# Forty residual additions of the second batch, moved from GpSimd instructions into accumulating transfers

## The chip, the cores and the metric

The kernel runs on one core of a Trainium2 chip. A core has five engines that run side by side, each with its own in-order queue of instructions: PE (TensorE, matrix products), DVE (VectorE), ACT (ScalarE), POOL (GpSimd) and SP (SyncE, which here only issues transfers). Sixteen DMA engines move data; any of the queues can issue to them, and PT<-Phl in the profile is a transfer that transposes on its way. The metric is device time in microseconds (us) for one execution, as the median of several runs.

## The reference, cut to what matters

The program is two layers over an input `x` of 2 batches x 1024 rows x 512 columns, in float32. In each layer an attention and a second branch both read a layer norm of `x`, and both results are added to `x`:

```
xn = layernorm(x)
x  = x + attn0(xn) + ffn0(xn)     # ffn0: four streams of 128 columns, mixed
xn = layernorm(x)
x  = x + attn1(xn) + ffn1(xn)     # attn1: 32 causal heads in 8 groups; ffn1: low-rank experts
```

The second branch of layer 0, `ffn0`, is what the change touches. Each row of 512 is seen as four streams of 128 columns. A small matrix `H_res` of 4x4 per row (made by 50 Sinkhorn steps) mixes the streams, and one branch result `y` of 128 columns is handed out to all four streams by weights `H_post`:

```
x_mixed[i]       = sum over j of H_res[i, j] * x_streams[j]
y_distributed[i] = y * H_post[i]
ffn0             = x_mixed + y_distributed
```

So for a block of 128 rows the residual gets one addition of 128x512 for `y_distributed`, and one addition of 128x512 for each of the four values of `j`.

## The kernel before

The rows are cut into 16 blocks of 128: `NT = 8` blocks for each of the two batches. The residual of block `t` of batch `b` stays on the chip for the whole program as `acc[b, t]`, 128 partitions x 512 float32. Products are done in float16 with a high and a low part, three passes for each (`mm3`, line 86).

The order of the whole program is: layer 0 of batch 0; layer 0's attention of batch 1; then layer 1, whose attention is one long loop (`layer1_attn`, line 807) over 16 groups (8 of batch 0, then 8 of batch 1) of 32 row steps each. Work that batch 1 still owes layer 0 is laid into the first groups of that loop with `put(h, s, f)` (line 1121), which gives a unit of work its row step. The program text sets the priorities; a list scheduler with a model of the time then writes the order of each engine's queue and places the semaphores and buffers. Two helpers correct it: `tc.issue_after` orders one engine's instructions, and `behind(i, j, True)` (line 195) makes instruction `i` wait for instruction `j` of another engine.

A row step (`row_step`, line 347) is the softmax of 128 rows: PE writes scores into PSUM (tile `s`), DVE subtracts a maximum (lines 292 and 296, tile `P`), ACT takes the exponential (line 300), DVE and ACT make the scale `r` (lines 324 and 325), ACT writes the high part (line 330, tile `Phl`) and DVE the low part (line 338, `Phl<-P,r,Phl`). The last DVE instruction of that kind is remembered in `last_low[0]`. POOL clears what is left of the tile (line 342), and SP issues the transposing transfer (line 343, `PT<-Phl`), which PE needs for the product with the values (line 373, tile `av`).

POOL does three other things in the loop. It issues the fetches of weights from HBM (`fetch`, line 715, into a tile tagged `f2k`); it splits them into high and low parts (`split_pool`, lines 97 to 99, `f2k` to `wq` or `wo`), each first instruction behind `last_low[0]`; and in the first part of the loop it does a Sinkhorn chain for batch 1 (lines 569 to 577, tile `sk`). Tiles tagged `f2k` share four buffers.

The additions of `ffn0` to the residual are done in two functions.

`branch0_add` (line 473) makes the 128x512 product of `y` and its four weights on POOL (line 477, into an `f2k` tile), and adds it to `acc[b, t]` on POOL (line 481). For batch 1 it is put at row steps 8, 10, ... 22 of the first group. The product, not the addition, is behind `last_low[0]` there.

`mix0_units` (line 624) does the mixing of one block: `load` fetches the input rows again into an `xr` tile and normalises them (on POOL at line 645 for batch 1), and four calls of `stream` follow, one for each `j`. With `pool` true (always for batch 1, four of the eight blocks of batch 0) ACT scales stream `j` four times into the four quarters of an `f2k` tile `m` (line 661), and POOL adds `m` to `acc[b, t]` (line 662). For batch 1 that addition too is behind `last_low[0]`. The units of batch 1 start at row steps 122 to 193 of the loop:

```
for t in range(NT):
    for k, f in enumerate(mix0_units(1, t, f0[1][5], True)):
        put(0, MX0 + MXN * (4 * t + max(k - 1, 0)) // 32, f)
```

What reads `acc[1, t]` next is the layer norm's statistics (`norm_stats`, line 217: DVE, line 219, `bnst<-acc`), once for each block, and later the normalised copy. In the same row steps the additions of layer 1's attention go to `acc[0, t]` (DVE, line 777), so they touch other blocks.

Of the kernel before, what the change touches and what calls it, by code (L numbers as in the profile page):

```python
# [12 lines left out]
ALU = mybir.AluOpType  # L13
# [41 lines left out]
def tile_model(ctx: ExitStack, tc: tile.TileContext, out: bass.AP, a: dict):  # L55
# [3 lines left out]
    V, A, G = nc.vector, nc.scalar, nc.gpsimd  # L59
# [7 lines left out]
    def T(tag, shape, dt=F32, bufs=None):  # L67
        count[0] += 1
        kw = {} if bufs is None else {"bufs": bufs}
        return sb.tile(shape, dt, tag=tag, name=f"{tag}_{count[0]}", **kw)  # L70
# [4 lines left out]
    def PP(shape=(P, 512)):  # L75
        count[0] += 1
        return ps.tile(list(shape), F32, tag="pp", name=f"pp_{count[0]}", bufs=BP)

    def bc(ap, axis, n):
        return ap.unsqueeze(axis).to_broadcast(  # L80
            [*ap.shape[:axis], n, *ap.shape[axis:]])
# [43 lines left out]
    acc = {}  # L125
# [60 lines left out]
    last_hi, last_lo, last_low = [None], [None], [None]  # L186

    def after(*insts):

        st = ExitStack()  # L190
        for i in insts:
            st.enter_context(tc.issue_after(i.ins))
        return st

    def behind(i, j, wait=False):

        kind = mybir.DependencyClass.Sync if wait else mybir.DependencyClass.NoSync
        tc.add_manual_dep(i.ins, j.ins.name, mybir.DependencyInfo(
            kind, mybir.DependencyReason.DATA), reason="behind")

    def rsqrt(y, ve, tag):

        t = T(tag, list(ve.shape), bufs=2)
        A.activation(t, ve, AF.Ln)
        A.activation(y, t, AF.Exp, scale=-0.5)
        V.tensor_tensor(t, y, y, ALU.mult)
        V.tensor_tensor(t, t, ve, ALU.mult)
        V.tensor_scalar(t, t, -0.5, 1.5, ALU.mult, ALU.add)
        V.tensor_tensor(y, y, t, ALU.mult)
# [51 lines left out]
    def srow():  # L261
        count[0] += 1
        return ps.tile([P, 512], F32, tag="s", name=f"s_{count[0]}", bufs=BS)
# [68 lines left out]
    def rows_lo(Pm, r, W, pool, hl, dst):  # L332
        whole, hi, los, pad = hl
        for a0, a1, lo in los:
            if pool:
                G.tensor_tensor(lo, Pm[:, a0:a1], hi[:, a0:a1], ALU.subtract)
            else:
                last_low[0] = V.scalar_tensor_tensor(lo, Pm[:, a0:a1], r[:, 1:2], hi[:, a0:a1],  # L338
                                                     ALU.mult, ALU.subtract)
        if pad is not None:  # L340

            behind(G.memset(pad, 0.0), last_low[0])  # L342
        nc.sync.dma_start_transpose(dst[:, :whole.shape[1] // P], whole)
# [129 lines left out]
    def branch0_add(b, t, y4, hh):  # L473

        y = y4
        y4 = T("f2k", [P, 4, P], bufs=FB)
        mul = G.tensor_tensor(y4, bc(y, 1, 4), bc(hh[:, t, 1, :], 2, P), ALU.mult)
        if b:
            behind(mul, last_low[0], True)
        af = acc[b, t]  # L480
        G.tensor_tensor(af, af, y4.rearrange("p i c -> p (i c)"), ALU.add)

    def attn0_rows(b, half, Q, K, between=lambda: None):
        PTs = []
# [139 lines left out]
    def mix0_units(b, t, rs, pool):  # L624


        got = {}

        def load():
            if b == 0 and t >= 4:  # L630
                if t % 2 == 0:
                    xr_more[t] = T("P", [P, 2, H], bufs=PB)
                xr = got["xr"] = xr_more[t & ~1][:, t % 2]
            else:
                xr = got["xr"] = T("xr", [P, H], bufs=XB)
            with after(t0):
                nc.sync.dma_start(xr, a["x"][(b * NT + t) * P:(b * NT + t + 1) * P, :])
            if b == 0:
                A.activation(xr, xr, AF.Identity, scale=rs[:, 2, t:t + 1], bias=rs[:, 1, t:t + 1])
                if not pool:  # L640
                    got["d"] = srow() if t < 4 else PP()
                    A.activation(got["d"], acc[b, t], AF.Copy)
                return
            with tc.issue_after(p0.ins):
                behind(G.tensor_scalar(xr, xr, rs[:, 2, t:t + 1], rs[:, 1, t:t + 1], ALU.mult, ALU.add),
                       last_low[0], True)

        def stream(j):
            if b == 0 and (not pool or j > 1):
                with after(*(last_rs[:1] if pool else last_rs[1:] if j else last_mix)):  # L650
                    stream_at(j)
            else:
                stream_at(j)

        def stream_at(j):
            xj = got["xr"][:, j * P:(j + 1) * P]
            by = [Hm[b][:, t, i, j:j + 1] for i in range(NC)]
            if pool:
                m = T("f2k", [P, H], bufs=FB)
                for i in range(NC):  # L660
                    A.activation(m[:, i * P:(i + 1) * P], xj, AF.Copy, scale=by[i])
                add = G.tensor_tensor(acc[b, t], acc[b, t], m, ALU.add)
                if b:
                    behind(add, last_low[0], True)
                return

            for i in range(NC):
                sl = slice(i * P, (i + 1) * P)
                dst = acc[b, t] if j == NC - 1 else got["d"]
                last_stt[0] = V.scalar_tensor_tensor(dst[:, sl], xj, by[i], got["d"][:, sl], ALU.mult, ALU.add)  # L670

        return [load] + [lambda j=j: stream(j) for j in range(NC)]
# [389 lines left out]
    for t in range(NT):  # L1062
        branch0_add(0, t, ys0[t], f0[0][4])
# [71 lines left out]
    for t in range(NT):  # L1135
        put(1, 2 * t, lambda t=t: branch0_add(1, t, y4s[t], f0[1][4]))
# [93 lines left out]
```

## Time and profile before

| what | us |
|---|---|
| median of 3 runs | 1851.93 (1847.24 to 1852.3) |
| the profiled execution's own time | 1847.82 |
| its span, first to last instruction | 1846.1 |
| PE busy | 1708.1 (93%) |
| DVE busy | 1473.8 (80%) |
| ACT busy | 1189.0 (64%) |
| POOL busy | 871.5 (47%) |

The batch 1 additions lie in two stretches. Those of line 481 start between 284.7 and 324.8 us, those of line 662 between 618.7 and 837.4 us. In the profile a line of a group reads: line, engine, operation, output tile <- input tiles, shapes, count | busy us, mean ns of one | idle time of the engine before them and what ended it. A line of the waits reads: who waited, at which line <- for whom: us in total, times, longest. A line of the stretches has the length of the stretch, then busy us and count for each engine, then TensorE's granted clock, the share of time that the DMA engines were busy, and GB/s. In the timeline a line has the start, the duration and the instruction. A DMA line ends with the us from issue to landing.

### The profile page before, as it was taken

Reading aid. Unit: us, or ns where it says so; the run is one execution under the profiler, and the core shown is the slowest. Engines: PE = TensorE matmul, PEld = TensorE weight load, DVE = VectorE, ACT = ScalarE, POOL = GpSimd, SP = SyncE. Lnnn points to the kernel's source line nnn. Section 1 sums busy time; section 2 is a strip of 40 time slices with the busy share of each in tenths; the row PEclk is TensorE's granted clock in tenths of the full one; section 3 lists DMA queues with packets and bytes.
Section 4 is the critical chain, followed back from the end, with each engine's and each line's share of the span. In section 5 each row is a group of like instructions: output and inputs, shape, how many; then the busy total and the mean of one; then the engine's idle time right before and its main releaser. Section 6 shows DMA issues by size and latency. Waiting matters only on the chain. (4 is left out here: it accounts for less than half of the span.)

```text
span 1846.1 us, 35011 instructions
## 1 busy us (share of the span) xinstructions
PE 1708.1 (93%) x11394; PEld 1038.2 (56%) x11394; DVE 1473.8 (80%) x4170; ACT 1189.0 (64%) x2917; POOL 871.5 (47%) x1460
## 2 busy tenths in 40 slices
PE   4666399999999999999999999999999999999998
PEld 2434146566666655566555566665666665665565
DVE  7988868888888877887577798898787877778675
ACT  3848656767665767886366667657566767666564
POOL 5568628878766464647254233324142323235200
PEclk9888699999999999999999999999999999999999
DMA  7435225756565656456484656557565665666455
GB/s 212 84 54 130 61 64 113 162 109 142 112 145 102 147 116 143 100 133 147 82 166 99 131 110 141 111 128 162 142 141 125 142 123 129 130 143 126 103 118 118
DMA packets 685034, 228.15 MB, mean 124 GB/s; under 512 B 665633, under 2 KB 665761, under 8 KB 684850
## 3 DMA queue, kind: packets, MB, share of 16 engines
q1 hardware_dynamic: 669394, 178.65, 47.2%
q0 software_dynamic: 13152, 43.07, 8.3%
q10 hardware_dynamic: 2304, 4.20, 0.7%
q8 instruction: 89, 1.46, 0.3%
q14 instruction: 95, 0.78, 0.2%
HBM read 52.81 MB, written 4.19 MB: 31 GB/s over the span
## 5 line engine op out<-in xcount | busy, mean ns | idle before, releaser
L300 ACT ACTIVATE P<-P,nm 128x1024 f32<-128x1024 f32 (+31 forms) x528 | 391.4, 742 | 278.1 <-DVE nm L292 253.4
L338 DVE SCALAR_TENSOR_TENSOR Phl<-P,r,Phl 128x64 f16<-128x64 f32 (+16 forms) x627 | 462.9, 763 | 79.0 <-ACT Phl L330 73.3
L91 PE MATMUL s<-K,Q 128*128 128x512 f16 (+22 forms) x2400 | 440.5, 317 | 19.8 <-DVE nm L292 10.5
L373 PE MATMUL av<-PT,V 128*128 128x256 f16 x3456 | 422.6, 273 | 12.2 <-DMA PT<-Phl 6.8
L373 PEld LDWEIGHTS <-V 128*128 128x128 f16 x3456 | 336.8, 98 | 95.1 <-DMA PT<-Phl 9.7
L330 ACT ACTIVATE Phl<-P,r 128x1024 f16<-128x1024 f32 (+31 forms) x515 | 368.8, 731 | 17.1 <-DMA PT<-Phl 2.0
L91 PE MATMUL pp<-wo,ao 128*128 128x512 f16 x1536 | 370.2, 380 | 3.3 <-ACT ao L107 3.2
L91 PE MATMUL pp<-big,wq 128*128 128x512 f16 x1536 | 368.6, 380 | 0.0
L97 POOL TENSOR_SCALAR f2k<-f2k 128x512 f32<-128x512 f32 x164 | 110.5, 675 | 512.3 <-DVE Phl L338 461.4
L91 PEld LDWEIGHTS <-Q 128*128 128x128 f16 x2400 | 223.9, 98 | 177.3 <-issue 29.6
L91 PEld LDWEIGHTS <-wq 128*128 128x128 f16 x1536 | 149.1, 98 | 166.8 <-issue 2.7
L91 PEld LDWEIGHTS <-ao 128*128 128x128 f16 x1536 | 149.7, 98 | 158.4 <-ACT ao L107 5.0
L91 PEld LDWEIGHTS <-big 128*128 128x128 f16 x1824 | 120.9, 99 | 87.8 <-DMA big<-wo 40.6
L292 DVE CUSTOM_DVE_ANT_0 P<-s,mask,nm 128x272 f32<-128x272 f32 (+15 forms) x256 | 157.7, 617 | 11.1 <-PE s L91 3.1
L296 DVE TENSOR_SCALAR_CACHE_REDUCE P<-s 128x512 f32<-128x512 f32 (+15 forms) x272 | 152.3, 562 | 11.9 <-PE s L91 10.4
L324 DVE RECIPROCAL r<-r 128x1 f32<-128x1 f32 x528 | 79.3, 155 | 78.6 <-ACT P L300 75.4
L325 ACT ACTIVATE r<-r 128x1 f32<-128x1 f32 x528 | 94.9, 192 | 68.3 <-DVE r L324 67.6
L107 ACT ACTIVATE ao<-av 128x512 f16<-128x512 f32 x128 | 75.0, 586 | 83.9 <-PE av L373 80.6
L342 POOL MEMSET Phl<- 128x192 f16 (+1 forms) x320 | 55.7, 189 | 153.0 <-DMA PT<-Phl 86.8
L292 DVE CUSTOM_DVE_ANT_0 P<-s,mask 128x32 f32<-128x32 f32 (+15 forms) x256 | 105.1, 430 | 19.0 <-PE s L91 18.6
L91 PE MATMUL pp<-big,big 128*128 128x128 f16 (+2 forms) x816 | 103.9, 283 | 17.5 <-DVE sk L606 12.7
L777 DVE SCALAR_TENSOR_TENSOR acc<-pp,acc 128x512 f32<-128x512 f32 x128 | 87.1, 681 | 31.6 <-PE pp L91 31.1
(266 smaller groups left out, 2064.3 us busy)
## 6 DMA issues: line engine op xcount, KB each, us to landing
f2k<-in_Wq POOLq DMA_DIRECT2D x64, 256.0 KB, 3.1
f2k<-in_WoT POOLq DMA_DIRECT2D x64, 256.0 KB, 3.3
PT<-Phl SPq DMA_TRANSPOSE x528, 3.2
acc<-in_x SPq DMA_DIRECT2D x16, 256.0 KB, 5.3
f2k<-in_Wup POOLq DMA_DIRECT2D x16, 256.0 KB, 3.4
xr<-V SPq DMA_DIRECT2D x32, 128.0 KB, 2.3
out<-acc ACTq DMA_DIRECT2D x16, 256.0 KB, 2.7
xr<-in_x SPq DMA_DIRECT2D x12, 256.0 KB, 5.1
```

What stands on the lines that cost most here:

```text
L91: nc.tensor.matmul(dst, lhs(l), rhs(r), start=(i == 0 and j == 0), stop=(i == n - 1 and j == 2))
L97: first = G.tensor_scalar(stage, stage, scale, 1.0, ALU.mult, ALU.mult)
L107: A.activation(hl_hi, src, AF.Copy, scale=scale)
L292: last_row[0] = V.tensor_tensor_reduce(Pm[:, o:o + w], pt[:, :w], mask[:, 512 - w:], -scale, first, ALU.add, ALU.min, nm[:, k:k + 1])
L296: last_row[0] = V.tensor_scalar(Pm[:, o:o + w], pt[:, :w], -scale, first, ALU.mult, ALU.min, accum_out=nm[:, k:k + 1])
L300: A.activation(Pm[:, :W], Pm[:, :W], AF.Exp, bias=last, scale=-1.0, accum_out=r[:, 0:1])
L324: V.reciprocal(r[:, 1:2], r[:, 0:1])
L325: A.activation(r[:, 1:2], r[:, 1:2], AF.Copy, scale=PSCALE)
L330: A.activation(hl[1], Pm[:, :W], AF.Copy, scale=r[:, 1:2])
L338: last_low[0] = V.scalar_tensor_tensor(lo, Pm[:, a0:a1], r[:, 1:2], hi[:, a0:a1], ALU.mult, ALU.subtract)
L373: nc.tensor.matmul(p, v, pt, start=(k == 0), stop=(k == len(todo) - 1))
L777: V.scalar_tensor_tensor(acc[b, t], p, 1.0 / 256.0, acc[b, t], ALU.mult, ALU.add)
```

## The change

A helper `add_to(dst, src)` issues a transfer from POOL's queue that adds `src` to `dst` where `dst` lies (both are on the chip). For batch 1, the addition of line 481 and the four additions of line 662 become such transfers: 8 + 32 = 40 in all, each 128 partitions x 512 float32 (256 KB). The wait of line 662's addition for the last low part goes with it; the product of line 477 keeps its own. Batch 0's additions stay POOL instructions, and the additions of the attention outputs stay on DVE.

```diff
+    def add_to(dst, src):
+
+        return G.dma_start(dst, src, accum_op=ALU.add)
+
     def rsqrt(y, ve, tag):
...
         if b:
             behind(mul, last_low[0], True)
-        af = acc[b, t]
-        G.tensor_tensor(af, af, y4.rearrange("p i c -> p (i c)"), ALU.add)
+        y4 = y4.rearrange("p i c -> p (i c)")
+        if b:
+            add_to(acc[b, t], y4)
+        else:
+            G.tensor_tensor(acc[b, t], acc[b, t], y4, ALU.add)
...
                     A.activation(m[:, i * P:(i + 1) * P], xj, AF.Copy, scale=by[i])
-                add = G.tensor_tensor(acc[b, t], acc[b, t], m, ALU.add)
                 if b:
-                    behind(add, last_low[0], True)
+                    add_to(acc[b, t], m)
+                else:
+                    G.tensor_tensor(acc[b, t], acc[b, t], m, ALU.add)
                 return
```

## The prediction

> **What bounds the kernel now.** I read the busy times and slices of the page first, then its chain, then stretches of the span, then the groups, waits and timeline of the stretch that the change touches.
>
> ```profile
> PE 1708.1 (93%) x11394; PEld 1038.2 (56%) x11394; DVE 1473.8 (80%) x4170; ACT 1189.0 (64%) x2917; POOL 871.5 (47%) x1460
> ...
> PE   4666399999999999999999999999999999999998
> ...
> PE 29%; DVE 3%; issue 1%; DMA 1%; ACT 1%; DVEq 0%; ACTq 0%
> ```
>
> From about 250 us on PE is the bound. A saving elsewhere counts only as far as it closes PE's holes. POOL is nowhere in the chain.
>
> ```profile
> core 0: us, PE busy (x) PEld busy (x) DVE busy (x) ACT busy (x) POOL busy (x), PEclk, DMA share, GB/s
> 280.00:330.00 50.00, 49.17 (x334) 30.49 (x333) 42.42 (x106) 33.08 (x82) 47.19 (x73) 1.00 0.57 125
> 400.00:617.00 217.00, 215.36 (x1419) 133.08 (x1418) 178.48 (x509) 141.55 (x338) 146.91 (x329) 1.00 0.59 122
> 617.00:840.00 223.00, 213.52 (x1501) 132.93 (x1499) 177.35 (x460) 174.59 (x472) 124.02 (x179) 1.00 0.60 132
> ```
>
> The mixing of batch 1 is the third stretch. PE misses 223.00 - 213.52 = 9.5 us there, against 217.00 - 215.36 = 1.6 in the one before: 7.8 more. In the first stretch (the branch sums) it misses 0.8. So 9.5 + 0.8 = 10.3 us is the most that these stretches can give back.
>
> ```profile
> L662 POOL TENSOR_TENSOR acc<-acc,f2k 128x512 f32<-128x512 f32 x32 | 42.9, 1342 | 61.9 <-DVE Phl L338 55.9 <-DVE r L324 4.0 <-ACT f2k L661 2.0
> ```
>
> ```profile
> PE s L91 <- DVE nm L292: 3.7, 4, 1.4
> PE av L373 <- DVE ao L108: 3.3, 2, 2.0
> ```
>
> These are the group of the 32 additions and PE's two longest waits between 617 and 840 us. With 0.6 more for DVE (`Q`) and 1.8 for ACT, 7.6 of 9.4 us are DVE's. POOL stood idle 59.9 us ahead of the additions, for DVE. The next lines are DVE's low parts alone (line 338) in the two long stretches, and the timeline at 750 us.
>
> ```profile
> 400.00:617.00 217.00, 61.06 (x72) 1.00 0.59 122
> 617.00:840.00 223.00, 72.85 (x72) 1.00 0.60 132
> ```
>
> ```profile
> 750.89 3.10 DVE L338 SCALAR_TENSOR_TENSOR Phl<-P,r,Phl 128x192 f16<-128x192 f32 x1
> 751.17 1.26 POOL L662 TENSOR_TENSOR acc<-acc,f2k 128x512 f32<-128x512 f32 x1
> ...
> 754.46 0.44 DVE L338 SCALAR_TENSOR_TENSOR Phl<-P,r,Phl 128x224 f16<-128x224 f32 x1
> ```
>
> The same 72 instructions take 11.8 us longer beside the additions. One of 192 columns took 3.10 us beside an addition and other POOL work; one of 224 took 0.44 without. The last lines are about transfers: three kinds and the software queue, and what follows a block's last addition.
>
> ```profile
> f2k<-in_Wq POOLq DMA_DIRECT2D x64, 256.0 KB, 3.1
> ...
> acc<-in_x SPq DMA_DIRECT2D x16, 256.0 KB, 5.3
> xr<-V SPq DMA_DIRECT2D x32, 128.0 KB, 2.3
> ```
>
> ```profile
> q0 software_dynamic: 13152, 43.07, 8.3%
> ```
>
> ```profile
> 837.39 1.26 POOL L662 TENSOR_TENSOR acc<-acc,f2k 128x512 f32<-128x512 f32 x1
> 839.43 0.68 DVE L219 BATCH_NORM_STATS2 bnst<-acc 128x6 f32<-128x512 f32 x1
> ```
>
> **The change, part by part.** The sum is made against the profiled execution, 1847.8 us (span 1846.1 and 1.7 around it), 4.1 below the median of 1851.9. I add the same difference to the median.
>
> *POOL's own time.* 32 additions (42.9 us) and 8 (11.4 us between 280 and 330) go; 40 issues come, at 0.59 us (the weight fetches on the same queue): 23.6. POOL is 30.7 us freer, worth nothing by itself: between 617 and 840 it is idle for 99 us, and around 300, where it has 47.19 of 50, PE has 49.17 of 50 all the same. Should an accumulating issue cost more than a fetch, the same idle time covers it: three times 0.59 for 32 would be 38 us more.
>
> *DVE's relief.* The low parts should lose up to 11.8 us. What a microsecond of DVE is worth at the end: 11.8 more of it stand beside 7.8 more of PE's holes, 0.66. But ACT also has 33 us more work there (174.6 against 141.6; the 128 scalings of line 661 are 40.3 and stay), so I give DVE half, 0.33: -3.9. Around 300 I take half of 0.8: -0.4. Bounds: 0 and -10.3.
>
> *When a transfer lands.* The trace shows no accumulating transfer. From below: 2.3 us (half the bytes, on the chip). From above: 8.2, the slowest of the loads into `acc`. I take 4.2, by the nearest row: a fetch of the same bytes on the same queue lands after 3.1 to 3.4, and a second read adds 0.9 (the software queue's 8.3% of 1846 us, over about 164 transfers). An addition took 1.3.
>
> *The wait that comes.* The four additions of a block change the same tile, so each waits on POOL until the one before has landed, and DVE's statistics wait for the last (as the first layer's wait for the loads into `acc` today: 8.2 us, 8 times). Today the statistics start 0.04, 2.6, 0.5, 0.4, 3.3, 1.2, 0.04 and 0.8 us after the last addition of their block. Block 4: additions at 736.6, 746.4, 748.4 and 751.2, statistics at 755.7. With 4.2 for each, the third goes at 750.6, the fourth at 754.8 and lands at 759.0, so DVE stands for 3.2 us, and the softmax queued behind with it. Over the eight blocks that makes 21.2 us if the transfers start where the additions do and DVE's order stays. If they start when ACT has written `m` (3.3 to 15.4 us earlier for the last of a block, as the wait for the low part is gone), it is 3.5 us. I take the middle, 12.4, times 0.33: +4.1. Bounds: 0 (2.3 us to land, early start) and 102 x 0.66 = +67 (8.2 to land, late start). The compiled order may put the statistics later by itself; nothing in the trace shows how far.
>
> *What is queued behind on POOL.* The waits inside a chain block POOL for 17.5 us (late start) to 78 (early), within its 99 idle plus the 24 freed there (42.9 less 18.9). Behind it stand the clearing of `Phl` (55 in this stretch), weight splits and fetches. The clearing holds up SP's transposes, and they PE; PE waited 0 for a transpose there and PEld 0.4, so there is room: +1.0, between 0 and +10 (at 8.2 us a chain blocks 109, beyond the idle time).
>
> *Buffers.* `m` is held from ACT's last write to the end of the addition: 6.3 us of waiting on average plus 1.3. A transfer without that wait holds it for 4.2 plus its chain, much the same; ACT waited 0.9 us for it. 0, bounds -0.9 and +5 (one more wait of 1.3 for every fourth of 32, half of it reaching PE).
>
> *The DMA engines.* 32 transfers at 2 x 0.9 us of sixteen engines are 60 in 223 us: the share goes from 0.60 to at most 0.87, beside the transposes. In slices with a share of 0.7 PE is at 9 tenths as in the others. 0, up to +3 if a transpose gets a microsecond later and one in 24 counts.
>
> [...] In the trace the additions follow each other on one engine, with a single wait of 0.2 us between two; no row shows what an overlap would lose. [...]
>
> Sum: -3.9 - 0.4 + 4.1 + 1.0 = +0.8. On the profiled run 1848.6, on the median **1852.7**: no change. About 0.3% (5.6 us) is what a measurement of this kernel can tell from none.
>
> **The rivals.**
> *Relief in full.* DVE's 11.8 us count at 0.66 and the holes around 300 close (-8.6), and every transfer lands ahead of its statistics. For it: POOL's 59.9 us of waiting goes, and ready streams were held 6.3 us. Against: ACT's load stays. 1843.3.
> *DVE waits for the landing.* If a transfer takes 5.3 us, as a load into `acc` does, the late start gives 40.4 us of waiting: 13.3 at 0.33, less 4.3, plus 1.0: +10.0, 1861.9; at 0.66 1875. It decides from where the relief of 4.3 is eaten (13 us of waiting) and is over 0.3% from 27 us, which is a landing of about 4.5 at a late start. For it: seven of eight statistics start within 3 us of the addition's end. Against: the early start.
> *The compiled order moves.* Different modelled durations may shift any queue after 285 us. After 850 PE's holes are 17.0 us (996 less 979.0); half of that either way is 1843 to 1860. Nothing in the trace decides it.
>
> **How the numbers follow.** No change 0.38; relief 0.21; late landing 0.29; moved order 0.12 (0.04 faster, 0.02 same, 0.06 slower). Faster 0.25, same 0.40, slower 0.35. The forecast's own range is 1846.4 to 1857.5. The range reaches from the bound of the relief (1851.9 - 10.3, rounded: 1842) to late landings between the two prices (1870); about 0.05 below and 0.12 above are left out.
>
> **What would show it.** Right: line 338 near 61 us for its 72 instructions while the streams are added; POOL down by some 30 us; statistics waiting for a DMA on `acc`, some 10 us in all; landings near 4.2; PE still at 9 in every slice. Wrong: landings over 5, DVE waits above 27 us, ACT waiting for `f2k`, or PE's holes moved to another stretch.

## The result, and the profile after

The changed kernel takes **1892.76 us** (median of 4 runs, 1890.38 to 1893.15) against 1850.77 for the kernel before (4 runs, 1847.24 to 1852.3). The ratio is **1.0227, 95% interval 1.0209 to 1.0245**: 42 us slower, where no change was forecast, and above the range. The profiled execution took 1890.38 us, its span 1888.6.

Lines of the page of the changed kernel: engines, PE by fortieths of the span, the chain, the new transfers (KB each, us from issue to landing) and the software queue.

```profile
PE 1723.8 (91%) x11394; PEld 1043.3 (55%) x11394; DVE 1456.4 (77%) x4170; ACT 1189.5 (63%) x2917; POOL 844.5 (45%) x1460
...
PE   4766389999999889898999999999999999999998
...
q0 software_dynamic: 18912, 53.56, 12.1%
...
PE 27%; DVE 2%; issue 1%; ACT 1%; DVEq 0%; ACTq 0%
...
acc<-f2k POOLq DMA_DIRECT2D x40, 256.0 KB, 4.0
```

POOL and DVE have become freer by 27.0 and 17.4 us, and the kernel slower. PE's slices show where: the new 8s, but for one near 240 us, stand between 610 and 900 us. Two stretches of the changed kernel, the first of all engines, the second of DVE's low parts alone (line 342, which was 338):

```profile
core 0: us, PE busy (x) PEld busy (x) DVE busy (x) ACT busy (x) POOL busy (x), PEclk, DMA share, GB/s
621.00:882.00 261.00, 228.29 (x1502) 138.18 (x1501) 165.57 (x470) 174.56 (x471) 108.69 (x183) 0.94 0.74 147
```

```profile
621.00:882.00 261.00, 58.09 (x73) 0.94 0.74 147
```

The same matrix products that took 223 us (617 to 840) now take 261. PE's holes there are 261.00 - 228.29 = 32.7 us (9.5 before), and the products themselves take 228.3 us instead of 213.5, at a granted clock of 0.94 instead of 1.00. So of the 38 us some 23 are holes and 15 are a lower clock. The low parts did lose what they lost to the additions: 72.85 us for 72 became 58.09 for 73.

From here on "the stretch" is one fixed piece of work in every kernel: the 1499 matrix products from the end of PE's 3323rd to the end of its 4822nd, worked out from the traces. It is 223.1 us before and 261.0 after. By the spans of the two profiled executions (42.5 us apart), 3.6 us more are lost ahead of it and 1.0 behind it. The 3.6 are there before the first moved addition: at PE's 1001st product (264.5 us before) the changed kernel is 5.8 us late.

The longest waits of the changed kernel between 617 and 875 us (who, at which line, for whom: us in all, times, longest):

```profile
PE s L91 <- DVE nm L296: 9.2, 5, 3.1
PE s L91 <- DVE Q L108: 4.0, 1, 4.0
...
DVE bnst L223 <- DMA acc<-f2k: 32.3, 8, 7.1
...
ACT P L304 <- DVE nm L296: 36.0, 12, 9.2
ACT f2k L668 <- DMA acc<-f2k: 18.9, 8, 5.8
...
POOL acc L203 <- DMA acc<-f2k: 29.6, 7, 5.8
```

Three engines now wait for a landing: DVE with all eight statistics, POOL with seven of the next transfers into the same tile, ACT for a free `f2k` buffer. Behind DVE stand ACT, with 36.0 us for DVE's maximum (19.1 before), and PE with 9.2 (3.7 before). One case, from the timeline of the changed kernel (start, duration, instruction, idle time ahead of it in brackets):

```profile
794.82 0.88 POOL L203 DMA_DIRECT2D acc<-f2k  x1 [5.61 <-DMA acc<-f2k]
...
798.06 0.69 DVE L223 BATCH_NORM_STATS2 bnst<-acc 128x6 f32<-128x512 f32 x1 [7.06 <-DMA acc<-f2k]
...
799.40 1.67 PE L91 MATMUL s<-K,Q 128*128 128x272 f16 x7 [4.00 <-DVE Q L108]
...
803.91 0.75 ACT L304 ACTIVATE P<-P,nm 128x544 f32<-128x544 f32 x1 [7.18 <-DVE nm L296]
```

The block's last transfer leaves at 794.82, 5.61 us late because it waits for the one before. The statistics stand at the head of DVE's queue for 7.06 us, `Q` is behind them, and PE stands still for 4.00 us. What follows the hole, by stretches of 5 us of the same kernel:

```profile
795.00:800.00 5.00, 1.00 (x10) 0.54 (x7) 1.94 (x5) 1.73 (x4) 2.31 (x5) 0.96 0.57 116
800.00:805.00 5.00, 5.00 (x33) 3.34 (x32) 4.85 (x15) 0.88 (x3) 2.92 (x4) 0.70 0.70 159
805.00:810.00 5.00, 5.00 (x42) 3.33 (x41) 2.82 (x6) 4.05 (x11) 2.02 (x4) 1.00 0.28 62
```

The granted clock is 0.70 in the five microseconds after it, and in the trace's clock records it is one half from 799.6 us on for 3.4 us. The stretch of the changed kernel has seven such spells, five of 3.4 us and two of 6.8, 30.7 us in all; the stretch of before has none. At half speed 30.7 us lose up to 15, which is what the products take longer. Each spell begins between 0.7 us before and 2.4 us after the end of one of PE's seven longest holes: 2.67, 2.71, 2.86, 2.92, 3.09, 3.99 and 4.00 us, 22.2 in all; the eighth is 1.28 us. The longest hole in the stretch of before is 2.04 us, and no spell follows it. What makes the clock fall isn't shown beyond that.

### The profile page after: what moved, and what is told of

Its sections match the earlier page's. It is cut to its first block, busy times and chain, and to the rows that moved or that the text cites. A ratio compares the mean times of both kernels' runs of the same rounds, so it can differ in the third digit from the quotient of the medians.

```text
span 1888.6 us, 35047 instructions
## 1 busy us (share of the span) xinstructions
PE 1723.8 (91%) x11394; PEld 1043.3 (55%) x11394; DVE 1456.4 (77%) x4170; ACT 1189.5 (63%) x2917; POOL 844.5 (45%) x1460
## 3 DMA queue, kind: packets, MB, share of 16 engines
q0 software_dynamic: 18912, 53.56, 12.1%
## 5 line engine op out<-in xcount | busy, mean ns | idle before, releaser
L342 DVE SCALAR_TENSOR_TENSOR Phl<-P,r,Phl 128x64 f16<-128x64 f32 (+16 forms) x627 | 444.4, 734 | 77.4 <-ACT Phl L334 69.0
L91 PE MATMUL s<-K,Q 128*128 128x512 f16 (+22 forms) x2400 | 444.7, 318 | 32.8 <-DVE P L300 14.9
L377 PE MATMUL av<-PT,V 128*128 128x256 f16 x3456 | 428.2, 276 | 11.0 <-DMA PT<-Phl 10.5
L346 POOL MEMSET Phl<- 128x192 f16 (+1 forms) x320 | 64.0, 229 | 156.7 <-DMA PT<-Phl 105.2
L91 PE MATMUL pp<-big,big 128*128 128x128 f16 (+2 forms) x816 | 103.4, 282 | 17.4 <-DMA big<-wo 16.8
```

The source lines that it names most:

```text
L91: nc.tensor.matmul(dst, lhs(l), rhs(r), start=(i == 0 and j == 0), stop=(i == n - 1 and j == 2))
L377: nc.tensor.matmul(p, v, pt, start=(k == 0), stop=(k == len(todo) - 1))
```

## The experiments

Four theories were set against each other: DVE waits with the **statistics** for a landing; the **chain** of four transfers into one tile blocks POOL's queue; the transfers' own **load** (53.56 MB on the software queue instead of 43.07, landings of 4.0 us beside 3.3 of a weight fetch and, by the author's estimate, a second read of the residual) holds up something else; the **buffers** tagged `f2k` run short. Against all of them stood the case that only the compiled order had moved. All ratios are to the kernel before, run on the same chip as the experiment (its medians there were 1848.8 to 1850.5 us).

| kernel | median us | ratio (95%) | stretch us |
|---|---|---|---|
| before | 1850.77 | 1 | 223.1 |
| after | 1892.76 | 1.0227 (1.0209 to 1.0245) | 261.0 |
| e1 after, statistics late | 1875.10 | 1.0148 (1.0122 to 1.0175) | 247.9 |
| e2 before, statistics late | 1843.43 | 0.9972 (0.9955 to 0.9989) | 216.2 |
| e3 branch sums only | 1853.90 | 1.0025 (1.0012 to 1.0039) | 224.1 |
| e4 streams only | 1887.09 | 1.0205 (1.0183 to 1.0226) | 259.5 |
| e5 = e1, two blocks in turn | 1863.86 | 1.0063 (1.0043 to 1.0083) | 237.2 |
| e6 = e1, streams to other blocks | 1866.11 | 1.0073 (1.0052 to 1.0094) | 238.7 |
| e7 = e1, plain copies | 1859.10 | 1.0043 (1.0030 to 1.0056) | 226.7 |
| e8 before, without the wait | 1842.29 | 0.9946 (0.9925 to 0.9967) | 215.7 |
| e9 = e5, five `f2k` buffers | 1874.22 | 1.0126 (1.0094 to 1.0158) | 237.9 |
| e10 = e1, five `f2k` buffers | 1888.55 | 1.0211 (1.0188 to 1.0233) | 248.3 |
| e11 = e2, five `f2k` buffers | 1870.29 | 1.0110 (1.0086 to 1.0134) | 220.2 |
| e12 = e8, statistics late | 1841.12 | 0.9947 (0.9928 to 0.9966) | 216.2 |
| e13 = e5, a quarter of the columns | 1851.38 | 1.0000 (0.9986 to 1.0013) | 222.4 |
| e14 = e5, plain copies | 1849.20 | 0.9988 (0.9970 to 1.0007) | 219.0 |
| e15 = e5, half of the transfers | 1849.69 | 0.9997 (0.9983 to 1.0010) | 218.2 |
| e16 = e12, two blocks in turn | 1841.82 | 0.9950 (0.9932 to 0.9968) | 215.7 |

The stretch is from one execution for each kernel. Those of e1 and e9 were 6.7 and 8.6 us above their kernels' medians, those of e5 and e10 3.6 and 2.3.

### e3 and e4: which of the two additions

e3 keeps the transfers of `branch0_add` and gives the streams their POOL addition and its wait back; e4 is the reverse.

```diff
 # e3, in stream
+                add = G.tensor_tensor(acc[b, t], acc[b, t], m, ALU.add)
                 if b:
-                    add_to(acc[b, t], m)
-                else:
-                    G.tensor_tensor(acc[b, t], acc[b, t], m, ALU.add)
+                    behind(add, last_low[0], True)
 # e4, in branch0_add
-        if b:
-            add_to(acc[b, t], y4)
-        else:
-            G.tensor_tensor(acc[b, t], acc[b, t], y4, ALU.add)
+        G.tensor_tensor(acc[b, t], acc[b, t], y4, ALU.add)
```

> Only the 8 branch sums are transfers; the 32 mixed streams are POOL additions with their wait, as before. Theories 1 and 2: no statistics and no chain near these 8, so 1851 to 1857 (the changed kernel was 3.8 us behind before the mixing began). Theory 3: may be anywhere from 1845 to 1890.

> Only the 32 mixed streams are transfers; the 8 branch sums are POOL additions as before. Theories 1 and 2: nearly the whole loss, 1884 to 1892. Theory 3: may be anywhere from 1845 to 1890.

The two parts add up: 0.25% is 4.6 us and 2.05% is 37.9, together 42.5 of 42. The stretch shows the streams' part alone (259.5 and 224.1). The time around the branch sums, first e3, then before, then after, in the same 65 us:

```profile
280.00:345.00 65.00, 61.70 (x391) 37.09 (x390) 53.94 (x135) 40.82 (x92) 53.38 (x96) 0.95 0.87 166
```

```profile
280.00:345.00 65.00, 63.51 (x419) 38.66 (x418) 54.89 (x138) 43.04 (x100) 58.39 (x96) 1.00 0.65 137
```

```profile
280.00:345.00 65.00, 62.66 (x418) 38.65 (x417) 53.76 (x150) 43.89 (x109) 55.39 (x98) 1.00 0.86 158
```

In e3 PE gets through 391 products instead of 419, after one hole of 3.3 us, with the granted clock at 0.95 and the share of the DMA engines at 0.87 instead of 0.65. But the changed kernel, with the same transfers and a share of 0.86, gets through 418; and e4, with no transfer there, through only 388, behind a hole of 4.5 us at the same product. By the start of the stretch e3 has caught up with before (616.3 and 616.8 us), and its profiled execution loses 4.0 of its 4.4 us behind the stretch. So the 4.6 us of the branch sums are a difference of whole runs; what makes it isn't shown.

### e1 and e2: the statistics later

`issue_after` keeps each block's statistics behind the low part that the program has reached. In the compiled queue of DVE they then stand behind 201 to 209 low parts instead of 129 to 194, so that every landing is over. e2 does the same to the kernel before, as a control.

```diff
-        norm_stats(1, ln1[1][0], t)
+        with tc.issue_after(last_low[0].ins):
+            norm_stats(1, ln1[1][0], t)
```

> The changed kernel, with each of batch 1's eight statistics queued on DVE behind the low part of its own row step (steps 198 to 205), so that DVE reaches them well after the last transfer of the block has landed. Theory 1 (DVE standing in front of the landing, 32.3 us in the profile, carries the loss): no wait of bnst for a transfer, 1852 to 1865 us, PE's granted clock back at 1.00 in the mixing. Theory 2 (the chain of transfers carries it: POOL blocked 29.6 us and ACT 18.9 us for f2k): those waits stay and the time stays above 1878. Theory 3 (the compiled order moved, whatever waits): the time need not follow the waits; above 1878 with few waits left would speak for it.

> The kernel before with the same queueing of the eight statistics and nothing else, as a control. Theories 1 and 2: 1851 plus or minus 6 us, as no transfer is waited for. Theory 3: a moved order by itself is worth 10 us or more either way.

In e1 DVE waits for no landing any more, and the stretch loses 13.1 of its 37.9 us. The larger part stays, and 1875 us lies between what the first two theories had said. e1's stretch, and its waits in it:

```profile
624.00:872.00 248.00, 219.70 (x1503) 135.37 (x1502) 160.06 (x449) 175.96 (x473) 111.15 (x185) 0.97 0.80 157
```

```profile
PE av L377 <- DMA PT<-Phl: 7.9, 3, 5.9
PE pp L91 <- POOL wo L98: 5.8, 1, 5.8
...
POOL acc L203 <- DMA acc<-f2k: 31.1, 9, 7.5
```

POOL stands in the chain for 31.1 us. PE now waits for what is queued behind it, a weight split of 5.8 us, and for a transpose. The control was faster than before by 0.28%, so late statistics are worth something without any transfer: e2's holes are 216.0 - 212.36 = 3.6 us.

### e5 and e6: no chain

e5 lays the streams of two blocks in turn, so that four transfers into one tile have others between them. e6 keeps the order and sends the four streams of a block to four different blocks, so its sums are not the program's.

```diff
 # e5
-            put(0, MX0 + MXN * (4 * t + max(k - 1, 0)) // 32, f)
+            put(0, MX0 + MXN * (8 * (t // 2) + 2 * max(k - 1, 0) + t % 2) // 32, f)
 # e6
-                    add_to(acc[b, t], m)
+                    add_to(acc[b, (t - 2 * j) % NT], m)
```

> The changed kernel with the statistics queued late (as in the first experiment, 1875 us) and the streams of two blocks put in turn (block 0 stream 0, block 1 stream 0, block 0 stream 1, ...), so that two transfers to the same block have another block's between them. All 40 transfers, their bytes and the rate of the streams stay. Theory 2 (the chain on one tile blocks POOL): POOL's wait for a transfer on acc falls from 31 to under 8 us and the time to 1845 to 1860. Theory 4 (the buffers: each transfer holds one of four f2k buffers for 4 us, and ACT stands for a buffer, 20.6 us): POOL's wait falls, ACT's stays at 15 to 25 us and the time above 1865. Theory 5 (the load on the DMA engines, or POOL's longer issue of 0.88 us): nothing changes, 1870 to 1880.

> The changed kernel with late statistics, and stream j of block t is added to block t - 2j (modulo 8) in place of block t, which makes the mixing wrong: the four transfers of a block are in four different tiles, and two to the same tile are some 50 us apart. Same order of the program, same transfers. Theory 2: no wait of POOL for a transfer on acc, 1845 to 1860. Theory 4: ACT's wait for f2k stays and with it the time, above 1865. Theory 5: 1870 to 1880.

Both take the chain away and come out alike (237.2 and 238.7 us of stretch): it was worth 10.7 and 9.2 us of the stretch. Both end near the line that had been drawn between the chain (up to 1860) and the buffers (above 1865). e5's stretch, and its waits:

```profile
621.00:858.00 237.00, 218.16 (x1500) 133.97 (x1499) 162.39 (x446) 174.71 (x471) 109.31 (x180) 0.98 0.83 161
```

```profile
POOL f2k L725 <- DMA acc<-f2k: 26.9, 10, 5.9
...
POOL acc L203 <- DMA acc<-f2k: 1.1, 1, 1.1
...
PE av L377 <- DMA PT<-Phl: 7.0, 2, 6.8
```

The wait of transfer for transfer is gone (31.1 to 1.1), and the weight split's hole too. What is left are waits for transfers: the fetch of the next weights waits for an `f2k` buffer that a transfer still reads, and PE waits for transposes, 10.4 us in e6. The slowest transpose in e5 lands after 10.9 us, where the slowest of e16, whose additions all stay on POOL, takes 5.8 and that of e12 7.1, worked out from its trace (min/median/max, first e5, then e16):

```profile
DMA to landing us min/median/max: 2.3/3.7/10.9
```

```profile
DMA to landing us min/median/max: 2.3/3.4/5.8
```

That transpose was issued at 637.5 us, 0.45 us ahead of an adding transfer that took 10.2. PE's hole of 6.8 us ends with it, and half clock lasts for 4.2 us more: by estimate some 9 us of the stretch from one late transpose.

### e7 and e14: a plain copy in place of the adding one

```diff
-                    add_to(acc[b, t], m)
+                    G.dma_start(acc[b, t], m)
```

> The changed kernel with late statistics, and the 32 streams are copied over the block instead of added to it (the addition of the streams is left out). Chain, buffers and bytes written stay; the second read and the adding go. Theories 2 and 4: landing 3.3 instead of 4.0 and issue 0.6 instead of 0.88, so the waits shrink by a fifth, 1866 to 1876. Theory 5 (DMA load or POOL's issue): back below 1860.

> The kernel of the fifth experiment with the 32 transfers copying over the block in place of adding (the addition of the streams is left out). If the adding, with its second read and its longer issue, is the remainder: 1843 to 1852. If moving 256 KB 32 times is enough by itself: 1856 to 1864.

These two leave the addition of the streams out. With the chain (e7 against e1) the plain copies make the stretch 21.2 us shorter, without it (e14 against e5) 18.2. Among plain copies the chain costs 7.7 (e7 against e14). A plain copy is issued in 0.55 us and lands after 2.9 to 3.1; an adding one is issued in some 0.9 and lands after 3.6 to 4.0 in the stretch (worked out from the traces). The second read was the author's estimate: the software queue carries 53.56 MB in e5 and in e14, at 11.8% and 10.5% of the engines' time. It is the adding that costs, and what of it is left to e13.

### e13 and e15: a quarter of the bytes, half of the transfers

```diff
 # e13
-                    add_to(acc[b, t], m)
+                    add_to(acc[b, t][:, 0:P], m[:, 0:P])
 # e15 (the other streams are added on POOL, without the wait)
-                if b:
+                if b and j % 2:
                     add_to(acc[b, t], m)
```

> The kernel of the fifth experiment (transfers, late statistics, two blocks in turn; 1864 us), and each of the 32 transfers adds only the first 128 of its 512 columns (three quarters of the mixing are left out): 64 KB in place of 256, same count, order and waits. Bytes beside the transposes (theory 5): transposes land after 3.5 us or less on average, 1843 to 1852. Count, issue and landing whatever the size: 1858 to 1866.

> The kernel of the fifth experiment with streams 1 and 3 as transfers, and streams 0 and 2 as POOL additions without the wait. If every transfer has its price: half of the 20 us, 1850 to 1857. If only crowding counts, less than a quarter of it: 1843 to 1848.

e13 leaves three quarters of each addition out. Its stretch, and how its two sizes of transfer land:

```profile
619.00:842.00 223.00, 214.80 (x1504) 132.86 (x1503) 164.70 (x447) 174.82 (x471) 109.24 (x181) 1.00 0.70 142
```

```profile
acc<-f2k POOLq DMA_DIRECT2D x8, 256.0 KB, 3.8
acc<-f2k POOLq DMA_DIRECT2D x32, 64.0 KB, 2.9
```

The number of transfers, their order and their issues (0.92 us each) are those of e5, and 14.8 of its 21.5 us above the control e16 are gone. So the issues can be at most the 6.7 us that are left. Whether the price goes with the number of transfers stays open: by the stretch half of them at full size (e15) leave 2.5 us above the control and all of them 21.5, but by ratio it is 8.7 and 20.9, with the branch sums in both. The 1849.69 us of e15 lie between the two ranges that had been named for it. With the bytes go three things: the engines' share (0.83 to 0.70), the transposes' mean landing in the stretch (4.20 to 3.67 us, worked out from the traces; 3.47 in e16) and the time that a buffer is held. The runs don't part them.

### e8, e12 and e16: the wait taken away, and no transfers

e8 is the kernel before without the wait of the streams' additions for a low part. e12 adds the late statistics, e16 also the two blocks in turn: they are the controls of e1 and e5.

```diff
                 add = G.tensor_tensor(acc[b, t], acc[b, t], m, ALU.add)
-                if b:
-                    behind(add, last_low[0], True)
                 return
```

> The kernel before without the wait of the 32 additions for the last low part, as the change drops it too: additions stay on POOL. If the dropped wait has a part in the loss (additions colliding with DVE's low parts, or a moved order): over 1854 us. If not: 1843 to 1854.

> No transfers: the kernel before without the wait of the 32 additions (1842 us in the eighth experiment) and with late statistics (1843 us in the second). If the two gains are of different waits they add: 1834 to 1840. If both only take away the same coupling of POOL to DVE: 1840 to 1845.

> Control: no transfers, POOL additions without their wait, late statistics (1841 us in the twelfth experiment) and two blocks in turn. If the turn by itself costs nothing: 1838 to 1846. If it is part of what remains of the fifth experiment's loss: over 1850.

e8 takes **1842.29 us, ratio 0.9946 (0.9925 to 0.9967)**, and so beats both kernels; e12 and e16 are no different from it. Its stretch, and the low parts in it:

```profile
622.00:838.00 216.00, 213.06 (x1503) 133.11 (x1502) 170.84 (x470) 174.72 (x473) 123.47 (x182) 1.00 0.63 138
```

```profile
622.00:838.00 216.00, 62.21 (x73) 1.00 0.63 138
```

PE's holes are 2.9 us. The low parts are back at 62.21 us for 73 with all 32 additions still on POOL. In the timelines 24 of the 72 low parts before run beside an addition, and 9 of the 73 in e8. In the same stretch of the changed kernel, with no addition on POOL, 73 take 58.09, and in e5 61.61: by this comparison the additions still cost DVE 0.6 to 4 us without the wait, and some 11 to 15 with it. Dropping the wait also frees POOL, which had stood 59.9 us for it; how much of the gain is that and how much DVE's isn't shown.

### e9, e10 and e11: one more buffer

```diff
-FB, PB, LB, XB, WB = 4, 3, 3, 4, 9
+FB, PB, LB, XB, WB = 5, 3, 3, 3, 9
```

> The kernel of the fifth experiment (transfers, late statistics, streams of two blocks in turn; 1864 us) with five f2k buffers in place of four, paid for with one xr buffer less. Theory 4 (transfers hold the f2k buffers, ACT and POOL's fetches stand for them: 19.2 and 26.9 us there): both waits fall to a third or less, and the time to 1843 to 1855. Theory 5 (DMA load, or the longer issue on POOL): 1858 to 1866.

> The kernel of the first experiment (transfers, late statistics, the four streams of a block one after another; 1875 us) with five f2k buffers and three xr. If buffers are the larger part of what is left there: 1850 to 1862, with POOL's wait for a transfer on acc (31 us) still there. If the chain on the tile is: 1866 to 1875.

> Control for the two runs before it: POOL additions as in the kernel before, late statistics (1843 us in the second experiment), five f2k and three xr buffers. Theories 4 and 5 alike: 1838 to 1848. Should it gain as much as the two with transfers do, the buffers are no part of the transfers' loss.

The fifth `f2k` buffer was paid for with one of the four `xr` buffers. ACT's wait for `f2k` falls from 20.6 us in e1 to this in e10:

```profile
ACT f2k L668 <- DMA acc<-f2k: 8.0, 4, 2.8
```

The stretch stays (247.9 and 248.3; 237.2 and 237.9), but that doesn't clear the buffers. All three kernels are slower in whole and outside every range named for them. The control's stretch grew by 4.0 us (216.2 to 220.2), so a gain of about 4 there may be hidden; by ratio the control lost 1.38% and the two with transfers 0.63%, a difference of 14 us that lies for the most part outside the stretch. In e9 the waits hardly fell (ACT 19.2 to 14.9 us, POOL's fetches 26.9 to 18.7), and in e10 POOL's wait in the chain rose from 31.1 to 39.2. A fifth buffer without the loss of an `xr` wasn't tried, so the buffers' part stays open.

### The sum

The transfers are best held against additions without the wait, since they have none. Ratio differences are turned into us with 1850.77; one ratio is good to 2 to 5 us, and a row of several to 4 to 8.

| compared | by ratio, us | by stretch, us |
|---|---|---|
| e8 - before: the wait dropped | -10.0 | -7.4 |
| after - e8 less e1 - e12: statistics wait for landings | +14.8 | +13.6 |
| e1 - e12 less e5 - e16: the chain | +16.3 | +10.2 |
| e5 - e13: three quarters of the bytes | +11.7 | +14.8 |
| e13 - e16: the rest, branch sums in the first column | +9.3 | +6.7 |
| sum: after - before | +42.0 | +37.9 |

The rows are rounded. The shares go by the order in which the causes were taken away; another order wasn't run. e1 stands in two rows: as far as its profiled execution was long within the stretch, the second column gives the chain too much and the statistics too little.

## Why the prediction was wrong

- **POOL's own time, 0.** Right in effect: POOL is 27.0 us freer and the kernel gains nothing by it. The issue costs 0.89 us, not 0.59; e13, with as many issues at 0.92, keeps only 6.7 of e5's 21.5 us above the control.
- **DVE's relief, -3.9 (bound -10.3).** The instructions lost a little more than was said (72.85 to 58.09 us, where 11.8 was forecast). The price looks too low: in e8, where low parts fell to 62.21, dropping the wait gave 10.0 us by ratio, which is near the bound, and 7.4 by stretch, though POOL's freedom is in that too. The gain of the rival of the relief in full is real, and it needs no transfer.
- **Landing, 4.2 us.** Measured 4.0. Right.
- **The wait that comes, 12.4 us of DVE, +4.1.** Mis-sized by a factor of 2.6: 32.3 us, and 13.6 to 14.8 us of time. The price of a DVE microsecond was near (13.6 / 32.3 = 0.42 against 0.33); the waiting was not. Even the late start in full had given 21.2. The transfers of a block follow each other some 4 us apart, and in the compiled queue seven of the eight statistics stood earlier than before (129 to 194 low parts ahead, instead of 132 to 197). The middle between two cases was taken where the order of a list scheduler could also go beyond both.
- **Queued behind on POOL, +1.0 (0 to +10).** The blocking of 29.6 us lay within the 17.5 to 78 forecast, and the step failed where it was called covered by idle time. The chain costs 10.2 by stretch, 16.3 by ratio. What came late was not the clearing of `Phl` but a weight split (5.8 us of PE in e1). There POOL's idle time didn't cover the wait, as the split in its queue was due.
- **Buffers, 0.** Neither confirmed nor refuted. That they would be held much the same was wrong: ACT's wait rose from 0.9 to 18.9 us. In e10 it fell by 12.6 us and the stretch stayed, but a buffer of another kind was taken away with it, which alone cost the control 4.0.
- **The DMA engines, 0 (up to +3).** The step that failed worst against its own bound: e13 and e14 put 14.8 and 18.2 us on the adding of full-size transfers. The share was foreseen (0.87 at most; 0.83 in e5). The cost of it was read from PE's slices before at a share of 0.7, and none of them had an adding transfer in it; the late transpose of e5 stood beside one. How much of the price is late transposes and how much the buffers isn't parted.
- **Around 300 us, -0.4.** The branch sums as transfers cost 4.6 by ratio (e3) in place of a gain. The profiles don't place it around 300 us, and its cause stays open.
- **No step for the clock.** Every hole was priced at its length. At each of the seven longest, of 2.7 to 4.0 us, the granted clock was one half for 3.4 us or more: 15 of the 38 us. It is part of the terms above, not beside them, and it is why the holes cost more than they measure.

Of what was named as a sign of being wrong, two came: DVE's waits above 27 us, and ACT waiting for `f2k`. The rival in which **DVE waits for the landing** had the right mechanism and its condition (over 27 us of waiting) was met, at a landing of 4.0 and not 5.3. Alone it ended at 1875 at most; chain and load came on top. That **the compiled order moves** explains little: behind the stretch the two kernels need the same time to within 1 us. No run left out the wait of a transfer for the landing of the one before into the same tile, so what an overlap of the two would do isn't shown.

## What to carry to other kernels

Before an engine's additions become transfers, count who will stand behind the landing: the next transfer into the same tile (here POOL, 29.6 us), the reader at the head of another engine's queue (DVE, 32.3), and the next user of the buffer (ACT, 18.9). In the changed kernel holes of 2.7 to 4.0 us in PE's work, 22 us together, cost 15 more in clock; in the stretch of before none of up to 2.0 us did. So the few long waits cost more than their own length there, and the shorter ones of before did not. And where an instruction is slow beside another engine's, look first at the wait that makes the two start together: dropping it gave 10.0 us here by ratio (e8), and moving the work lost 42.

## What was not expected of the hardware

- An adding transfer of 256 KB within the chip took POOL 0.89 us to issue and 4.0 to land; a plain one 0.55 and about 3.
- Beside 32 adding transfers in the stretch (e5) the slowest transpose took 10.9 us, against 5.8, 6.5 and 7.1 in three kernels without them (e16, before, e12). A quarter of the bytes in as many transfers left 6.7 us of the 21.5 above the control.
- With PE holes of 2.7 to 4.0 us the granted clock went to one half, for 3.4 us five times and for 6.8 twice. In e5 and e6 a spell also followed several holes of 0.5 to 1.4 us close together (worked out from the traces).
- DVE's low parts took 72.85 us for 72 beside the POOL additions with the wait for a low part, and 62.21 for 73 beside the same additions without it (e8); with no addition on POOL 73 took 58.09 in the changed kernel and 61.61 in e5.
